# A four-layer graph network: block 1 is turned behind block 0 in layer zero, its products follow the second unit, and layer one's prologue gets a second square buffer

## The chip, the cores and the metric

The kernel runs on one core of one Trainium2 chip. TensorE (PE) multiplies matrices into PSUM, VectorE (DVE), ScalarE (ACT) and GpSimd (POOL) work element by element, and SyncE (SP) issues most of the transfers. The metric is device time in microseconds of one launch; a time is the median of several executions. One further execution was recorded by the hardware profiler. Its clock starts at the start of the recorded span.

## The reference, cut to what matters

Four graph layers run one after the other over 4096 nodes with 256 features each, under one dense 4096 x 4096 adjacency of 0 and 1. Each layer computes new features from the neighbours, adds them to the old ones and normalises each row.

```python
# layer 0: additive attention, 4 heads       x = layernorm(x + elu(softmax(leaky(s_i + s_j), masked) @ (x @ W)))
# layer 1: dot-product attention, 4 heads    q, k, v = x @ Wq + bq, x @ Wk + bk, x @ Wv + bv
#                                            x = layernorm(x + softmax(q k^T / 8 + mask^T) @ v)
# layer 2: additive attention, 1 head        as layer 0, with one head and another slope
# layer 3: cosine attention                  x = layernorm(0.5 * softmax(cos(k, q), masked) @ x + 1.5 * x)
x = _layernorm(x + _L0_gnn_ref(x, adj, L0_gnn_W, L0_gnn_a), axis=-1)
x = _layernorm(x + _L1_gnn_ref(x, adj, L1_gnn_Wq, ...), axis=-1)
```

All of it is float32. Layers are counted from zero here, as in the names of the inputs; the change's own short description counts layer 1 of the code as the second.

## The kernel before, in words

The features stay in SBUF as `X`, 32 tiles of 128 rows, in eight blocks of four tiles (512 rows). A product that contracts over the features needs a block turned, so that features lie on partitions. There are two ways of turning one in this kernel. `transposed_block` (L112) does it with eight PE transposes of 128 x 128 into two PSUM banks, each copied out into `xT` by an engine that the caller names. `turning_apart` (L122), called through `block_apart` (L151), does it without PE: DVE transposes 32 x 32 squares into a buffer `squares` (two instructions, L129), one DMA writes that to DRAM (`far`, L133), and four DMAs read it back with the squares in their turned places (L137).

**Layer zero** (`additive_heads`) goes over units (block b of targets, tile j of sources), 8 x 32 of them. For a unit, `weights` (L291) lets ACT compute four heads of unnormalised weights from a broadcast row (L299, four instructions), and DVE adds one and multiplies by the mask (L302, one instruction of 128 x 2048). `sums` (L305) then multiplies the values of tile j with these weights on PE (L312), two units later (`LAG = 2`). Ahead of that stand the values. For each block, `turn` (L354) turns the features and asks for the load of the block after next, and `prepare` (L361) calls `additive_values` (L208): PE multiplies with the weights `w_sb` (L215; three tiles into the PSUM tile `side`, one into another bank), ACT takes three exponentials of each part (L219 to L221) and DVE scales the values (L222, one instruction for three tiles and one for the fourth).

The start is written out. PE runs two small products of ones (`warm`, L377), broadcasts `a_row` into `side`, DVE attaches the attention vectors to the weights (L107, L109), block 0 is turned, two more products of ones follow, block 0's values are prepared, and `first_rows` (L267) broadcasts block 0's source terms into four banks: one of its own and three of the PSUM tile `over`. The first unit's weights read these banks, and `keep_rows` (L275) copies them into SBUF, two by ACT and two by DVE (L277). Then block 1 is turned into two banks of `side`, and the loop begins. In step i = 0, behind unit 0's weights, block 2 is turned and block 1 prepared.

**Layer one** (`multi_head_attention`) begins with projections. `keys(b)` multiplies block b by Wk and Wq on PE (L738), ACT adds the bias (L746), and DVE takes the greatest absolute value of each part (L747). `values(b)` does the same for Wv (L757, L764). Between `keys(0)` and `keys(1)` stands `tail`, the end of layer zero's last block: DVE divides and takes negatives (L329, L331, L229), ACT the exponential (L230), DVE adds and normalises. Block 1 is turned on PE with copies by ACT (L119), blocks 2 to 7 through DRAM, with one buffer for `squares` (pool `mh_sq`, L718), two for `far` and four for `xT`. Then come 8 x 64 units of attention. Layers two and three follow; neither is touched.

PE's order is the order of the code wherever `manual_schedule` names PE, which covers both places. The order on DVE, ACT and SP in these two places is chosen when the kernel is built, by a scheduler that places the instructions by estimated readiness. [...] A tile of a pool can be written again when the last reader of its former content is done.

## Time and profile before

| | us |
|---|---|
| median of 3 executions | 2790.39 (2789.6 to 2793.18) |
| profiled execution, its own time | 2791.86 |
| its span | 2790.1 |
| PE busy | 2772.4 |
| DVE busy | 2286.1 |
| ACT busy | 1702.6 |
| POOL busy | 1051.2 |
| layer zero's products begin | 19.37 |
| layer one's projections begin | 722.69 |
| layer one's attention begins | 812.45 |

The granted TensorE clock was 0.999 over the profiled execution. In a timeline of the profile each row gives the start, the length, the engine, the line, the operation, what it writes and reads, and in brackets the idle time of that engine just before it with what ended this. A list of waits gives the sum, the number of times and the longest. A 32-bit product appears as two records, a transpose as one.

### The profile page before, as it was taken

To read this page: it belongs to the slowest core of one execution; us is meant where nothing else is said; L and a number is where in the kernel's file an instruction comes from. 1 tells how busy PE (TensorE), PEld (TensorE's weight loads), DVE (VectorE), ACT (ScalarE), POOL (GpSimd) and SP (SyncE) were. 2 spreads that over 40 slices of the span, in tenths; PEclk is the share of its full clock that TensorE was granted. 3 is DMA by queue.
4 is the path that set the end of the run, shared out by engine and by line. 5 is a ranking of instruction groups with operands and counts; after the bars stand their busy time and mean duration, and the time that the engine had idled before them with its cause. 6 is when DMAs were issued, how large, how long until landed. Compare 5 with 4: busy or idle time off the path is not lost. (4 is left out here: it accounts for less than half of the span.)

```text
span 2790.1 us, 50215 instructions
## 1 busy us (share of the span) xinstructions
PE 2772.4 (99%) x19445; PEld 1427.4 (51%) x19445; DVE 2286.1 (82%) x3055; ACT 1702.6 (61%) x2665; POOL 1051.2 (38%) x986
## 2 busy tenths in 40 slices
PE   9999999999999999999999999999999999999999
PEld 5333333333453333333333333688888777777776
DVE  8899999999677788887888888888887877767676
ACT  8899999999336666666666666465565422222222
POOL 0000001100029878778788784355455000000000
PEclk9999999999999999999999999999999999999999
DMA  7566676665339899998989988567777545445442
GB/s 209 109 140 137 139 145 132 135 142 114 69 97 193 184 179 196 192 188 183 195 181 190 191 182 187 169 195 215 186 210 232 117 77 82 76 68 83 75 72 43
DMA packets 275065, 411.92 MB, mean 148 GB/s; under 512 B 54809, under 2 KB 155657, under 8 KB 273930
## 3 DMA queue, kind: packets, MB, share of 16 engines
q0 software_dynamic: 104176, 182.74, 41.3%
q1 hardware_dynamic: 164280, 218.88, 26.3%
q10 hardware_dynamic: 6370, 7.10, 0.7%
q8 instruction: 152, 2.49, 0.4%
q14 instruction: 87, 0.71, 0.1%
HBM read 335.94 MB, written 39.40 MB: 135 GB/s over the span
## 5 line engine op out<-in xcount | busy, mean ns | idle before, releaser
L837 DVE TENSOR_TENSOR prob<-p,mask 128x1024 f32<-128x1024 f32 x512 | 619.8, 1222 | 166.9 <-ACT p L827 160.7
L827 ACT ACTIVATE p<-p,shift 128x1024 f32<-128x1024 f32 x512 | 555.6, 1088 | 318.9 <-PE p L825 318.7
L312 PE MATMUL acc<-prob,V 128*32 128x512 f32 x6144 | 664.0, 592 | 1.2 <-DVE prob L302 1.2
L299 ACT ACTIVATE prob<-row,dst 128x512 f32<-128x512 f32 x1020 | 635.1, 712 | 0.6
L302 DVE SCALAR_TENSOR_TENSOR prob<-prob,mask 128x2048 f32<-128x2048 f32 x256 | 580.4, 2286 | 25.8 <-ACT prob L299 25.2
L847 POOL TENSOR_TENSOR den<-den,prob 128x1024 f32<-128x1024 f32 x220 | 558.2, 2537 | 91.1 <-DVE prob L837 84.1
L825 PE MATMUL p<-qT,kT 64*64 64x512 f32 x4096 | 531.1, 590 | 1.6 <-DVE prob L837 1.6
L861 PE MATMUL acc<-prob,V 64*64 64x512 f32 x4096 | 529.9, 589 | 0.0
L312 PEld LDWEIGHTS acc<-prob,V 128*32 128x32 f32 x6144 | 197.3, 110 | 453.0 <-issue 431.6
L446 PE MATMUL acc<-mix,mixed 128*128 128x256 f32 x1428 | 388.6, 380 | 4.3 <-DVE mix L437 1.3
L861 PEld LDWEIGHTS acc<-prob,V 64*64 64x64 f32 x4096 | 157.4, 133 | 282.1 <-issue 280.3
L825 PEld LDWEIGHTS p<-qT,kT 64*64 64x64 f32 x4096 | 154.3, 133 | 278.6 <-issue 256.1
L446 PEld LDWEIGHTS acc<-mix,mixed 128*128 128x128 f32 x1428 | 269.3, 190 | 47.6 <-PE acc L446 3.5
L90 POOL COPY tick<-prob 128x1 f32<-128x1 f32 x35 | 38.0, 1085 | 642.1 <-DVE prob L302 641.2
L1133 DVE TENSOR_TENSOR prob<-prob,mask 128x1024 f32<-128x1024 f32 x128 | 156.1, 1219 | 145.9 <-ACT prob L1125 145.8
L853 POOL DMA_DIRECT2D den<-prob x240 | 230.3, 960 | 62.5 <-DMA den<-prob 22.3
L1053 POOL DMA_DIRECT2D mask<-in_adjT x64 | 47.6, 743 | 530.5 <-DVE prob L1133 442.4
L446 PE MATMUL acc<-prob,X 128*128 128x256 f32 x952 | 244.3, 379 | 0.0
L446 PEld LDWEIGHTS acc<-prob,X 128*128 128x128 f32 x952 | 180.8, 190 | 78.1 <-issue 56.4
L569 DVE SCALAR_TENSOR_TENSOR prob<-r,own,mask 128x512 f32<-128x512 f32 x252 | 177.1, 743 | 51.4 <-POOL s L169 13.6
L1125 ACT ACTIVATE prob<-p 128x512 f32<-128x512 f32 x144 | 86.1, 598 | 204.0 <-PE p L1121 204.0
L1125 ACT ACTIVATE prob<-g 128x512 f32<-128x512 f32 x112 | 66.9, 597 | 208.0 <-PE g L1121 208.0
(236 smaller groups left out, 2821.9 us busy)
## 6 DMA issues: line engine op xcount, KB each, us to landing
mask<-in_adjT SPq DMA_DIRECT2D x254, 512.0 KB
den<-prob POOLq DMA_DIRECT2D x240, 512.0 KB, 5.3
mask<-edges SPq DMA_DIRECT2D x512, 64.0 KB
mask<-in_adjT POOLq DMA_DIRECT2D x64, 512.0 KB, 5.7
edges<-in_adj POOLq DMA_DIRECT2D x32, 512.0 KB, 9.6
far<-squares SPq DMA_DIRECT2D x16, 512.0 KB
den<-prob SPq DMA_DIRECT2D x16, 512.0 KB
row<-far SPq DMA_DIRECT2D x7, 1024.0 KB
```

What stands on the lines that cost most here:

```text
L299: nc.scalar.activation(z[:, h, :], r, AF.Relu, bias=-1.0, scale=dst[:, j, h:h + 1])
L302: nc.vector.scalar_tensor_tensor(z, z, 1.0, mask[m][:, j % MJ, :].unsqueeze(1).to_broadcast([P, H, QW]), OP.add, OP.mult)
L312: nc.tensor.matmul(acc[b][h * G:(h + 1) * G, n, :], part, prob[b, j][:, h, :], start=(j == 0), stop=(j == NT - 1))
L446: nc.tensor.matmul(acc[at][:, half * HW:(half + 1) * HW], w, a, start=(g == 0 and n in (0, 2, 3, 5)), stop=(g == NP - 1), skip_group_check ...
L569: nc.vector.scalar_tensor_tensor(z[:, n, :], r, ga.own[:, j:j + 1], mask[:, n, :], OP.add, OP.mult)
L825: nc.tensor.matmul(p[c * d:(c + 1) * d, r, :], kT[half, c, at:at + d], qT[half, c, cols], start=True, stop=True)
L827: nc.scalar.activation(p, p, AF.Exp, bias=shift)
L837: nc.vector.tensor_tensor(z, p, mask[m][:, j % MJ, :].unsqueeze(1).to_broadcast([P, KC, QW]), OP.mult)
L847: nc.gpsimd.tensor_tensor(to, to, flat, OP.add)
L853: nc.gpsimd.dma_start(to, flat, accum_op=OP.add)
L861: nc.tensor.matmul(acc[b][c][r * d:(r + 1) * d, :], V[half, j, r * d:(r + 1) * d], prob[b, j][half, r, :], start=(j == 0), stop=(j == NH - 1))
L1133: nc.vector.tensor_tensor(z, z, co.mask[b, 2 * g // MJ][:, lo:lo + 2, :], OP.mult)
```

## The change

Block 1's transposes move up behind block 0's, into two banks of `over`, in the place of the second pair of warm-up products; these two go. Both of its copies out of PSUM go to ACT, where they were DVE's. In the loop, turning block 2 and preparing block 1 move from step i = 0 to step i = 1, so in the code they stand behind the second unit's weights. The first products (`sums`) still come in step 2, so that PE's own order from `first_rows` on stays, but for the eight transposes that have moved. In layer one's prologue the pool of the square buffers gets two buffers.

```diff
--- before.py
+++ after.py
@@ -354,8 +354,7 @@
             def turn(b, bank=bank):
                 if b + 2 < NB:
                     load_x(b + 2)
-                busy = (nc.scalar.copy if b == 0 else nc.vector.tensor_copy,
-                        nc.vector.tensor_copy if b == 1 else nc.scalar.copy)
+                busy = (nc.scalar.copy if b < 2 else nc.vector.tensor_copy, nc.scalar.copy)
                 xTs[b] = transposed_block(sb, bank, b, busy)
 
             def prepare(b):
@@ -380,12 +379,11 @@
                 nc.tensor.matmul(side[:, 0, :], ones[:1, :], a_row, start=True, stop=True)
                 attach(keep, w_sb, side[:, 0, :], H)
                 turn(0)
-                warm(2)
+                free = iter([over[:, 1, :], over[:, 2, :]])
+                turn(1, lambda: next(free))
                 prepare(0)
                 banks = [bank()] + [over[:, h, :] for h in range(H - 1)]
                 first_rows(banks)
-                free = iter([side[:, 0, :], side[:, 1, :]])
-                turn(1, lambda: next(free))
                 for i in range(len(units) + LAG):
                     if i < len(units):
                         b, j = units[i]
@@ -400,8 +398,8 @@
                         if b:
                             finish(b - 1, j)
 
-                    if i == 0 or i % QB == 3 and 3 + i // QB <= NB:
-                        b = 1 if i == 0 else 2 + i // QB
+                    if i == 1 or i % QB == 3 and 3 + i // QB <= NB:
+                        b = 1 if i == 1 else 2 + i // QB
                         if b + 1 < NB:
                             turn(b + 1)
                         prepare(b)
@@ -715,7 +713,7 @@
             with ExitStack() as pro:
                 wp = pool(pro, "mh_w", 1)
                 sb = pool(pro, "mh_in", 4)
-                sq = pool(pro, "mh_sq", 1)
+                sq = pool(pro, "mh_sq", 2)
                 own = pool(pro, "mh_o", 2)
                 dr = pool(pro, "mh_far", 2, space=bass.MemoryType.DRAM)
                 ps = pool(pro, "mh_ps", 6, space=PSUM)
```

In the order built from this, DVE's copies of block 1 are gone, its copy of block 2 stands ahead of the first copied row, and the scaled values of block 1's fourth tile stand behind unit 1's mask step. In layer one's prologue the squares of blocks 3, 4 and 5 stand ahead of the first reciprocal of layer zero's last block, where only block 3's stood, and SP has the square writes of blocks 2 to 5 ahead of the reads of block 2, where it had those of blocks 2 and 3. What follows is unchanged on every engine.

## The prediction

> **What bounds the kernel now.** I read the page first, for the engine that is never idle. Its part on busy time:

> ```profile
> PE 2772.4 (99%) x19445; PEld 1427.4 (51%) x19445; DVE 2286.1 (82%) x3055; ACT 1702.6 (61%) x2665; POOL 1051.2 (38%) x986
> ```

> TensorE (PE) is busy for 2772.4 of 2790.1 us: 17.7 us of idle time in all. Only moving PE's few waits can change the time. So the second view is the list of PE's waits (in total, times, longest); four touch the edited places:

> ```profile
> PE g L738 <- ACT xT L119: 1.4, 1, 1.4
> ...
> PE acc L312 <- DVE prob L302: 1.2, 1, 1.2
> ...
> PE acc L215 <- DVE xT L119: 0.5, 1, 0.5
> PE pv L757 <- DVE V L764: 0.3, 1, 0.3
> ```

> Two lie in the first 26 us, two in layer one's projections near 737 us. The third view is the timeline of each engine there. PE at the start (start, length, engine, operation; idle time before it in brackets):

> ```profile
> 4.26 2.05 PE L117 MATMUL g<-ident,X 128*128 128x128 f32 x8
> 6.11 1.06 PE L377 MATMUL acc<-ones 128*128 128x128 f32 x4
> 7.45 3.12 PE L215 MATMUL acc<-w_sb,xT 128*128 128x264 f32 x12 [0.29 <-issue]
> ...
> 13.19 1.04 PE L117 MATMUL acc<-ident,X 128*128 128x128 f32 x8
> ...
> 23.30 2.78 PE L312 MATMUL acc<-prob,V 128*32 128x512 f32 x24 [1.16 <-DVE prob L302]
> ```

> The same eight transposes take 2.05 us at 4.26 and 1.04 us at 13.19. The last row is the one that matters: unit 1's products wait for VectorE's mask step (L302). VectorE (DVE) up to it:

> ```profile
> 14.27 1.29 DVE L119 COPY xT<-acc 128x512 f32<-128x512 f32 x2 [2.01 <-PE acc L117]
> 15.77 0.69 DVE L277 COPY row<-acc 128x512 f32<-128x512 f32 x1 [0.21 <-ACT prob L299]
> 16.37 2.28 DVE L302 SCALAR_TENSOR_TENSOR prob<-prob,mask 128x2048 f32<-128x2048 f32 x1
> 18.57 0.69 DVE L277 COPY row<-acc 128x512 f32<-128x512 f32 x1
> 19.17 0.68 DVE L119 COPY xT<-g 128x512 f32<-128x512 f32 x1
> 19.77 0.95 DVE L222 TENSOR_TENSOR V<-acc,V 128x768 f32<-128x768 f32 x1
> 20.64 0.42 DVE L222 TENSOR_TENSOR V<-g,V 128x256 f32<-128x256 f32 x1
> ```

> Unit 1's mask step follows at 20.97. In layer one, DVE, ACT and PE around PE's 1.4 us wait:

> ```profile
> 732.44 1.30 DVE L129 STREAM_TRANSPOSE squares<-X 128x512 f32<-128x512 f32 x2 [6.26 <-DMA far<-squares]
> 733.67 0.64 DVE L747 TENSOR_REDUCE kbig<-kT 128x1 f32<-128x512 f32 x1
> ...
> 735.97 0.28 DVE L229 TENSOR_SCALAR neg<-o 128x256 f32<-128x256 f32 x1
> ...
> 736.28 0.42 ACT L230 ACTIVATE neg<-neg 128x256 f32<-128x256 f32 x1 [5.33 <-DVE neg L229]
> 736.61 1.05 ACT L119 COPY xT<-g 128x512 f32<-128x512 f32 x2
> ...
> 737.23 3.70 PE L738 MATMUL g<-xT,wk_sb 128*128 128x512 f32 x8 [1.36 <-ACT xT L119]
> ```

> DVE sits 6.26 us because block 3's squares need the one square buffer, which block 2's write to DRAM still reads. DVE's negatives of layer zero's last block stand behind it, ScalarE's (ACT) exponential behind those, ACT's copies of block 1's features behind that, and PE at the end.

> [...] (2.05 against 1.04 us), so transposes put in place of the second warm-up keep the array as busy, and run slow. [...] GpSimd's transfer of the first mask, issued at 723.11 and landing 6.7 us later, fills the engines while block 2's squares wait; these move at up to 469 GB/s only from about 728 and land by 732.4. [...]

> **The change part by part**, with the built order of each engine: PE changes only at the start; in layer one DVE and SP change, ACT does not.

> Start, PE. Out goes the second warm-up (6.11 to 7.17, and 0.29 idle); eight transposes of block 1 come in, and leave their place at 13.19, a saving of 0.88 us there (to the next at 14.07). They need block 1's load, third on SP's queue. The DMA rates of the first microseconds sum to the 1.31 MB of block 0, w0 and block 1 at about 6.2 us; with some landing time, 6.4. At the cold pace 1.85 us to the next instruction: block 0's products start at 8.25 and not 7.45. Their first group took 3.12 us against 2.84 later, so 0.2 comes back: first rows 0.6 us later (0.2 if the load is there at 6.11, 1.5 if it lands at 7.3).

> Start, ACT and DVE. Two copies (2 x 0.59) go to ACT, which is idle from 6.94 to 10.61: free. DVE loses 2 x 0.69, which delayed nothing but the row copy at 15.77 by little, as that then waited for ACT. Unit 0's mask step follows ACT's weights: 16.37 + 0.6 = 16.97. From unit 0's to unit 1's mask step DVE takes 4.60 us now. Afterwards block 2's copy stands before the first row copy, in time that DVE waits anyway, and the one-tile V product behind unit 1's mask step (this is what products behind the second weights do; PE's own order there stays). Left: 2.20 + 0.60 + 0.87 = 3.67. Unit 1's mask step: 20.64 against 20.97, **0.3 us gained** (bounds: 0.7 gained, 0.6 lost). PE has no further wait until layer one's projections, so this reaches them whole.

> Layer one. With two buffers block 3's squares (two of 0.61) follow block 2's at once, at 724.7, during DVE's idle time: free. But in the built order blocks 4's and 5's squares come forward too, before the reciprocal at 734.82. Block 4's need the landing of block 2's write, so they start at 732.44, as block 3's did. Block 5's need block 3's write. That is issued near 726.1 and not 733.8; its data goes right behind block 2's, so about 733.6, and DVE asks at 734.24: no further wait. So four transposes stand behind the old wait where two stood: 2 x 0.61 = 1.22 us more ahead of DVE's negatives, and every link to PE is exposed. PE's wait grows from 1.36 to about 2.6: **1.2 us lost**. Bounds: nothing lost and 1.36 gained, if block 2's write lands 2.6 us earlier; 1.8 lost if block 3's write takes as long as the uncrowded ones (2.4 us from issue at 756.08 to use at 758.81) after block 2's landing. PE's 0.3 us wait moves with DVE and stays. Later squares (1.57 and 3.58 us of DVE waits) go; no PE wait stood behind those.

> SP is the queue passed. It issues four square writes and then 16 reads, each instruction in turn, instead of two and eight. Block 2's reads go from 734.29 to about 736. Ahead of them 1.05 MB of blocks 4 and 5 and then their own 0.52 at some 230 GB/s (what that queue moved from 734 to 740): landed by about 743, and PE wants them at 748.57. Free, with 6 us of cover.

> The sum: -0.3 + 1.2 = +0.9 us on a span of 2790.1. The profiled execution took 2791.86, the median is 2790.39: **2791.3 us**, no change that can be told, since 0.2% (5.6 us) is about what a measurement of this kernel tells from no change; the three runs alone spread over 3.6.

> **Rivals.** (a) The wait leaves layer one: block 2's write lands early enough that four transposes end before PE notices. For: block 3's write no longer starts late, and POOL's mask is not tied to it. Against: the first mask's issue follows PE's last product of layer zero in both kernels. Price: -0.3 - 1.4 = 2788.7. (b) The start loses: block 1's load lands near 8, first rows come 2 us later and unit 1's mask step 1.1 us later: +1.1 + 1.2 = 2792.7. For: the load shares the engines with w0; against: the sum of bytes above. (c) Slower: block 3's write is held up behind two transfers, and DVE's second wait goes to PE one to one. It decides the sign when the write lands 4.7 us after 734.24, at 739; at 740 the time is 0.9 + 5.8, 2797.1. For: block 2's took 7.65 us from its issue; against: the mask that held it is done by 729.8. (d) The edit does nothing: the second buffer is never used ahead. The built order speaks against it; the start's +-0.5 alone would be left, 2790.1.

> **How the numbers follow.** The forecast 0.60 (its own range, with the scatter of runs, 2789.5 to 2793); (a) 0.12, (b) 0.13, (d) 0.05: all within 0.2%. (c) 0.07. Something faster by over 0.2% that no wait here allows (the four waits and the warm-up sum to 4.5 us): 0.03. So faster 0.03, same 0.90, slower 0.07. Range 2788.6 to 2794.5: it takes in (a), (b) and the bounds of the forecast, and leaves (c) out.

> **What would show it.** Right: PE's wait at L738 near 2.6 us; in layer one DVE's wait on the squares' write ending near 732.4, followed by two transposes, a reduction and two more; unit 1's products starting near 23.0 with no wait at block 1's products. Wrong: a second DVE wait between the square pairs (c), a PE wait at the second eight transposes above 1 us (b), L738 without a wait (a), any new wait after 749 us, where I expect none.

## The result: 2796.9 us, slower by some 2 to 5 us, and the profile after

| | before | after | ratio after/before |
|---|---|---|---|
| first comparison, median of 12 and 12 executions, us | 2791.52 (2789.47 to 2796.3) | 2796.94 (2792.9 to 2799.79) | 1.0016 [1.0009, 1.0024] |
| the changed kernel once more, median of 31 and 19, us | 2793.36 (2789.74 to 2799.25) | 2796.92 (2792.45 to 2800.41) | 1.0008 [1.0001, 1.0015] |
| profiled execution, its own time, us | 2791.86 | 2795.52 | |
| its span, us | 2790.1 | 2793.7 | |

The change makes the kernel slower, by 0.08% to 0.16%, which is 2.2 to 4.5 us; the medians lie 3.6 and 5.4 us apart. That is inside the 0.2% named as no change, but both intervals exclude 1. The predicted 2791.3 is below every execution of the changed kernel, and the range ended at 2794.5. The two profiled executions differ by 3.7 us where 0.9 was forecast, so 2.8 us must be found in the trace. Part of the miss against 2791.3 is not the change at all: the median of the unchanged kernel was 2790.39 in the three executions that the prediction had, and 2791.52, 2794.54 and 2793.36 in the later comparisons.

Busy time, from the page of the changed kernel:

```profile
PE 2773.0 (99%) x19441; PEld 1427.6 (51%) x19441; DVE 2289.1 (82%) x3053; ACT 1703.8 (61%) x2667; POOL 1052.7 (38%) x986
```

PE is busy for 0.6 us more than before, and idle for 2793.7 - 2773.0 = 20.7 us in place of 17.7. So most of the loss is waits. The list of PE's waits of the changed kernel (total, times, longest):

```profile
PE g L736 <- ACT xT L119: 2.3, 1, 2.3
PE acc L117 <- DMA X<-in_x: 2.0, 1, 2.0
PE acc L312 <- DVE row L277: 1.5, 1, 1.5
```

L736 is the former L738. Its wait grew from 1.36 to 2.30 us, near the 2.6 foreseen. A wait on block 1's load (L117), for which the forecast had a landing at 6.4 us and so some 0.3, is 2.0 us, and unit 0's products have a new wait of 1.5 us. PE's timeline of the changed kernel, over both places:

```profile
4.21 1.97 PE L117 MATMUL g<-ident,X 128*128 128x128 f32 x8
8.21 1.97 PE L117 MATMUL acc<-ident,X 128*128 128x128 f32 x8 [2.02 <-DMA X<-in_x]
9.97 3.65 PE L215 MATMUL acc<-w_sb,xT 128*128 128x264 f32 x12
...
22.36 2.78 PE L312 MATMUL acc<-prob,V 128*32 128x512 f32 x24 [1.52 <-DVE row L277]
25.59 2.78 PE L312 MATMUL acc<-prob,V 128*32 128x512 f32 x24 [0.45 <-DVE prob L302]
...
740.46 3.70 PE L736 MATMUL g<-xT,wk_sb 128*128 128x512 f32 x8 [2.30 <-ACT xT L119]
```

Read the starts against those before. Block 0's products: 9.97 for 7.45, 2.5 us late. Unit 1's products: 25.59 for 23.30, 2.3 late. Keys of block 1: 740.46 for 737.23, 3.2 late. The spans: 3.6. So nearly two thirds of the loss arise in the first 26 us, one more microsecond at L736, and the rest is within what PE's small waits change from one execution to the next. Now DVE, in the same execution:

```profile
18.81 0.69 DVE L277 COPY row<-acc 128x512 f32<-128x512 f32 x1 [1.24 <-ACT prob L299]
19.42 2.28 DVE L302 SCALAR_TENSOR_TENSOR prob<-prob,mask 128x2048 f32<-128x2048 f32 x1
21.62 0.68 DVE L277 COPY row<-acc 128x512 f32<-128x512 f32 x1
22.22 0.95 DVE L222 TENSOR_TENSOR V<-acc,V 128x768 f32<-128x768 f32 x1
23.24 2.29 DVE L302 SCALAR_TENSOR_TENSOR prob<-prob,mask 128x2048 f32<-128x2048 f32 x1
...
734.49 1.31 DVE L129 STREAM_TRANSPOSE squares<-X 128x512 f32<-128x512 f32 x2 [5.69 <-DMA far<-squares]
735.72 0.64 DVE L745 TENSOR_REDUCE kbig<-kT 128x1 f32<-128x512 f32 x1
736.28 1.29 DVE L129 STREAM_TRANSPOSE squares<-X 128x512 f32<-128x512 f32 x2
...
739.20 0.28 DVE L229 TENSOR_SCALAR neg<-o 128x256 f32<-128x256 f32 x1
```

Unit 0's mask step begins at 19.42 and not at 16.37; unit 1's follows 3.82 us later and not 4.60. The second copy of a row (21.62) is what unit 0's products wait for, because their tile takes the place of `over` in the pool, and that copy reads from `over`. This wait costs nothing by itself, since unit 1's products wait for unit 1's mask step in either case. In layer one four transposes stand behind the old wait, in the order foreseen: two, a reduction, and two more without a second wait. DVE ran nothing of what stood behind the first pair while it waited for 5.69 us.

### The profile page after: what moved, and what is told of

It is laid out like the page before. It is cut to its first block, busy times and chain, and to the rows that moved or that the text cites. A ratio compares the mean times of both kernels' runs of the same rounds, so it can differ in the third digit from the quotient of the medians.

```text
span 2793.7 us, 50203 instructions
## 1 busy us (share of the span) xinstructions
PE 2773.0 (99%) x19441; PEld 1427.6 (51%) x19441; DVE 2289.1 (82%) x3053; ACT 1703.8 (61%) x2667; POOL 1052.7 (38%) x986
## 5 line engine op out<-in xcount | busy, mean ns | idle before, releaser
L312 PE MATMUL acc<-prob,V 128*32 128x512 f32 x6144 | 664.0, 592 | 2.0 <-DVE row L277 1.5
L299 ACT ACTIVATE prob<-row,dst 128x512 f32<-128x512 f32 x1020 | 634.8, 712 | 0.6
L302 DVE SCALAR_TENSOR_TENSOR prob<-prob,mask 128x2048 f32<-128x2048 f32 x256 | 580.5, 2286 | 25.6 <-ACT prob L299 24.8
L312 PEld LDWEIGHTS acc<-prob,V 128*32 128x32 f32 x6144 | 197.3, 110 | 453.9 <-issue 431.6
```

Of the source, the lines that this page charges most:

```text
L299: nc.scalar.activation(z[:, h, :], r, AF.Relu, bias=-1.0, scale=dst[:, j, h:h + 1])
L302: nc.vector.scalar_tensor_tensor(z, z, 1.0, mask[m][:, j % MJ, :].unsqueeze(1).to_broadcast([P, H, QW]), OP.add, OP.mult)
L312: nc.tensor.matmul(acc[b][h * G:(h + 1) * G, n, :], part, prob[b, j][:, h, :], start=(j == 0), stop=(j == NT - 1))
```

## The experiments

In the tables of starts, "unit 1" is the start of unit 1's products, the point where the start of the kernel hands its delay on to everything after. Single executions come with one time each; their verdict rests on the trace, not on that time.

### The two halves of the change apart

The start alone is the changed kernel with one square buffer, as the diff has it; the squares alone are the kernel before with two, the same line the other way round.

```diff
-                sq = pool(pro, "mh_sq", 2)
+                sq = pool(pro, "mh_sq", 1)
```

> The changed start with one square buffer. Theory A (two separate losses: block 1's load lands near 8.2 us and costs about 2.3 us at the start, the squares moved ahead cost about 0.9 in layer one): PE waits 1.5 to 2.5 us before the second eight transposes, unit 1's products start near 25.6 against 23.3, the wait at layer one's second keys stays at 1.4, and the median is 2.3 us over before. Rival B (the start costs only what one execution happened to show, and the rest of the 5.4 us between the medians comes with the second buffer, or from a stage that neither edit touches): no more than 1 us over before.

> The old start with two square buffers. Theory A: the first 26 us as before, PE's wait at layer one's second keys 2.3 us against 1.4, the median 0.9 us over before. Rival B: 3 us or more over before, with idle time of PE that lies outside the first 26 us and the projections.

PE's timelines of the start alone, and of the squares alone:

```profile
7.78 1.97 PE L117 MATMUL acc<-ident,X 128*128 128x128 f32 x8 [1.26 <-DMA X<-in_x]
9.55 3.86 PE L215 MATMUL acc<-w_sb,xT 128*128 128x264 f32 x12
...
25.36 2.78 PE L312 MATMUL acc<-prob,V 128*32 128x512 f32 x24 [0.44 <-DVE prob L302]
```

```profile
738.43 5.33 PE L738 MATMUL g<-xT,wk_sb 128*128 128x512 f32 x8 [2.53 <-ACT xT L119]
...
750.49 3.60 PE L738 MATMUL g<-xT,wk_sb 128*128 128x512 f32 x8
```

| | unit 1 | wait at the second keys | second keys |
|---|---|---|---|
| before | 23.30 | 1.36 | 737.23 |
| start alone | 25.36 | 1.20 | 739.13 |
| squares alone | 23.33 | 2.53 | 738.43 |
| both | 25.59 | 2.30 | 740.46 |

By the second keys the start has lost 1.90 us, the squares 1.20, and both 3.23: they nearly add up. The squares' 1.2 us is the forecast's figure.

One execution says little of a start, so take all of them: unit 1's products begin at 23.30 to 24.70 in the five executions with the start as before (23.76 in the mean), and at 25.36 to 27.00 in the three with the changed one (25.98). The two groups don't overlap, and the 2.2 us between their means is the start's loss as the traces show it. The timed medians can't confirm losses of this size: 2794.73 for the start alone (14 executions), 2794.67 for the squares alone (13), against 2794.54 (27) for the kernel before on the same chip, ratios 1.0000 [0.9993, 1.0008] and 1.0004 [0.9997, 1.0012]. An interval of 0.0015 is 4 us wide. The 2.3 us over before that was expected of the start alone is not in its median, which is 0.2 us over; it lies at the upper end of the interval, some 2.2 us. What follows rests on the traces.

The squares alone lost more behind the second keys. These took 5.33 us and not 3.70, since the granted clock was 0.50 from 738.33 to 741.74, and the third keys begin at 750.49 against 748.57: 1.92 us lost by then. In every trace here the changes of the granted clock lie whole multiples of 3.413 us apart (one from 738.33 to 741.74; 814 from full pace at 7.89 us to half clock at 2786.33, after PE's last work, in the kernel before, and 814 from 11.61 to 2790.06 in the changed one); call that a step. The step before this one held 2.43 us of PE idle time. The start alone shows the same once, far from both edits: 2.68 us of idle time in one step, then half clock from 2510.17 to 2513.58. No other step between full pace and PE's last work holds more than 1.81 us in any of the fourteen profiled executions, and none of them was followed by half clock. The waits of the changed kernel at L736, 2.30 and 2.97 us, each fell across two steps, and no half clock followed. So such a wait can cost more in one execution than in another. How often it does in the timed executions is not shown.

### Is it the early turn, or the order on DVE

The start alone again, with block 0's products ahead of block 1's turn. The second warm-up stays away.

```diff
                 turn(0)
+                prepare(0)
                 free = iter([over[:, 1, :], over[:, 2, :]])
                 turn(1, lambda: next(free))
-                prepare(0)
```

> The changed start, one square buffer, but block 1 is turned behind block 0's products and not ahead of them. Theory A (the load is late): PE no longer waits for a load; the products of block 0 start at about 7.4, the turning costs 0.9 us ahead of the first rows, and unit 1's products start at 23.0 to 23.6. If the loss came from the copies on ScalarE instead, they would hold unit 0's weights as before, and unit 1's products would still start after 25.

```profile
7.46 4.97 PE L215 MATMUL acc<-w_sb,xT 128*128 128x264 f32 x12 [1.08 <-ACT xT L119]
...
25.65 2.78 PE L312 MATMUL acc<-prob,V 128*32 128x512 f32 x24 [0.44 <-DVE prob L302]
```

No wait for the load is left, the products start where they did before (7.46), and still unit 1 begins at 25.65. The twelve records took 4.97 us, where before they took 3.12. The load's wait was thus only one way to lose those 2 us. Here PE stood idle for 1.08 us where the warm-up had been, and full pace, seen in the single records of the trace (0.223 us for a record of 264 columns instead of 0.44), began at 11.55 us instead of 7.96. By itself this start after 25 us also fits the rival named beforehand, that block 1's copies on ACT hold up unit 0's weights; the run with the warm-up put back, further down, has the same copies and answers it.

### The load with nothing behind it

The start alone, with no later load of features, mask or edges issued until DVE has attached the attention vectors to the weights (a small DVE copy of these into block 2's place opens the queue again, at 8.31 us). The core of the edit; the first masks and edges are held in the same way:

```diff
-                if b + 2 < NB:
-                    load_x(b + 2)
+                if 1 < b < NB - 2:
+                    with tc.issue_after(first[0]):
+                        load_x(b + 2)
```

> The changed start, one square buffer; the loads of blocks 2 and 3, of the first mask and of all that follows wait until VectorE has attached the vectors to the weights (about 8 us), so that nothing stands on SP's queue behind block 1's load. If that load is late because later loads share the DMA engines with it, it lands at 6.3 to 6.8 and PE waits 0.6 us at most. If it is late because its sixteen parts run on engines of unequal progress whatever follows, PE still waits 1.5 to 2.2 us. Units 0 and 1 may start later here, as their mask and block 2 come later.

```profile
6.99 1.97 PE L117 MATMUL acc<-ident,X 128*128 128x128 f32 x8 [0.68 <-DMA X<-in_x]
8.75 4.17 PE L215 MATMUL acc<-w_sb,xT 128*128 128x264 f32 x12
...
24.89 2.78 PE L319 MATMUL acc<-prob,V 128*32 128x512 f32 x24 [0.44 <-DVE prob L309]
```

With the queue to itself, block 1's load lets the transposes begin at 6.99 us; with the later loads behind it, at 7.78, 8.21 and 8.58 in the three executions that waited for it with the queue unchanged. In the second of these, the first profile of the changed kernel, the load's sixteen parts landed from 6.21 to 8.16 us. PE's wait is 0.68 us, where at most 0.6 was expected if the later loads are the cause, and 1.5 to 2.2 if they are not. So, by this one execution, between 0.8 and 1.6 us of its lateness are the transfers behind it. What remains is 0.8 us over the 6.2 us of the sum of bytes; the queue moved next to nothing after 6.3 us, so some 0.7 us lie between the last bytes and their first use. But unit 1's products begin at 24.89, only 0.47 us sooner than in the start alone, since the twelve records now took 4.17 us: full pace came at 11.65.

### The warm-up put back

First, the order with block 0's products ahead, and `warm(2)` back in front of them, as the diff has it. Second, the start alone with only a `warm(4)` added between the two turns, so that PE is busy while the load is awaited.

```diff
                 turn(0)
+                warm(2)
+                prepare(0)
                 free = iter([over[:, 1, :], over[:, 2, :]])
                 turn(1, lambda: next(free))
-                prepare(0)
```

> As the run with the later turning, one square buffer, and the second pair of warm-up products is back ahead of block 0's products. Theory A (the idle microsecond before about 7.9 us costs TensorE its full pace until about 11.4): block 0's first twelve records take 3.1 us again and not 4.97, first rows start at 12.2 to 12.4 and not 14.03, unit 1's products at 23.6 to 24.0 and not 25.65. Theory B (those records were slow because they waited for the weights or for a copy): no more than 0.5 us earlier than without the warm-up.

> The changed start with block 1 turned ahead of block 0's products, one square buffer, and four warm-up products between the two turnings, to keep TensorE busy while block 1's load is under way. Theory A: the load still decides when the second turning starts (7.5 to 8.3), but that takes 1.0 us and not 2.0, and block 0's first twelve records 2.9 to 3.1 and not 3.65; unit 1's products start at 23.8 to 24.5, against 25.4 to 25.6. Theory B: the same as without them, 25.4 to 25.6.

PE's timelines, the first and the second:

```profile
6.38 1.06 PE L376 MATMUL acc<-ones 128*128 128x128 f32 x4
7.38 2.91 PE L215 MATMUL acc<-w_sb,xT 128*128 128x264 f32 x12
...
23.52 2.78 PE L312 MATMUL acc<-prob,V 128*32 128x512 f32 x24 [0.45 <-DVE prob L302]
```

```profile
6.33 1.92 PE L376 MATMUL acc<-ones 128*128 128x128 f32 x8
8.04 1.91 PE L117 MATMUL acc<-ident,X 128*128 128x128 f32 x8
9.74 3.14 PE L215 MATMUL acc<-w_sb,xT 128*128 128x264 f32 x12
...
24.85 2.78 PE L312 MATMUL acc<-prob,V 128*32 128x512 f32 x24 [0.44 <-DVE prob L302]
```

With 1.06 us of filler back and block 1's turn behind the products, unit 1 begins at 23.52 instead of 25.65: nearly all of the start's loss is gone (before: 23.30), in an execution whose full pace came early, at 7.38, the earliest of all. ACT makes the same copies here, so these were not what held the start. In the second, no PE gap is left, and the records take 3.14 us in place of 3.86. Yet unit 1 begins at 24.85, later than the 23.8 to 24.5 expected, as full pace came only at 10.18 us: a PE that is always busy is not all that it hangs on.

### Do transposes bring PE to full pace

The kernel before, with forty transposes of block 0's tiles, read by nobody, in place of the second warm-up.

```diff
-                warm(2)
+                for k in range(40):
+                    nc.tensor.transpose(over[:, 0, k % QB * P:(k % QB + 1) * P], X[:, k % QB, :P], ident)
```

> The kernel before, with forty transposes of block 0's tiles (whose results nothing reads) in place of the second warm-up. No instruction of PE waits for a load between 4.2 us and the products. Full pace has begun at 7.4 to 11.3 us in the eight executions whose PE had no gap before the first products, and at 11.55 to 13.9 us in the five that had one. Theory one, the gap of PE delays full pace and transposes keep the array as busy as products do: the forty begin near 6.3 us at 0.213 us each, and somewhere between 7.4 and 11.3 us they go over to 0.107 us; they are done between 10.7 and 13.1 us, and block 0's first twelve product records come at full pace, in about 2.8 us. Theory two, [...] all forty take 0.213 us, 8.5 us in all, the products begin near 14.8 us, and full pace comes only 1.7 to 4.1 us after that, so that the twelve records take 3.6 to 5 us. The time itself is 3 to 10 us over that of the kernel before.

```profile
6.37 5.18 PE L384 MATMUL acc<-ident,X 128*128 128x128 f32 x40
11.38 2.84 PE L215 MATMUL acc<-w_sb,xT 128*128 128x264 f32 x12
```

All forty at the slow pace would be 8.5 us. They took 5.18: the first seven come 0.213 us apart, from about 7.7 us on they are 0.109 us apart, and the products run at full pace from their first record. So in this execution PE went over to full pace in the middle of a row of transposes, after 3.5 us of nothing but transposes (4.22 to 7.7 us). The price is clear too: the single time is 2796.89 against 2792.01, with unit 1 at 26.95.

The records give the moment of full pace, to within one record, in each of the fourteen profiled executions. Nine had no gap over 0.5 us before the first products: 7.38, 7.7, 7.96, 7.99, 8.36, 8.87, 10.18, 10.43, 11.34. Five had a gap of 0.68 to 2.33 us there: 11.55, 11.65, 11.67, 11.68, 13.86. The two groups don't overlap. The clock's change to full pace is on record too, so the steps of 3.413 us seen above can be counted back from it in each execution. The step that ended with this change held at most 0.32 us of PE idle time in all fourteen, and at most 0.65 us of the one-row product that broadcasts `a_row`. Every step before it held at least 0.42 us of idle time or at least 0.69 us of that product. So full pace came at the end of the first step that PE had filled almost wholly with other work. No step with a gap of 0.7 us or more inside it ended with that change. Where the steps begin differed from one execution to the next: less whole steps, the fourteen moments above lie some 0.2 to 3.4 us after the start of the span. This is read from fourteen records with narrow margins, and no run could set where the steps begin.

### The squares kept out of DVE's way

The kernel before with two square buffers, and the squares of blocks 4 and later allowed only after the step that ends layer zero's last block (`ends` holds the instructions that scale a finished row).

```diff
-                            xTs[b + 1] = block_apart(sb, sq, dr, b + 1, nc.sync)
+                            with tc.issue_after(ends[-1]) if b > 2 else nullcontext():
+                                xTs[b + 1] = block_apart(sb, sq, dr, b + 1, nc.sync)
```

> The old start and two square buffers, but the squares of blocks 4 and on are queued on VectorE behind the last scaled row of layer zero's last block. If the loss in layer one is the four transposes and the old wait ahead of the negatives: VectorE waits for no transfer there, the wait of 1.4 us at layer one's second keys (2.5 with two buffers) is gone or under 0.3, and the second keys start at 735.9 and not 737.2. If it is something else about the second buffer, 2.3 us or more remain.

```profile
725.46 1.89 DVE L129 STREAM_TRANSPOSE squares<-X 128x512 f32<-128x512 f32 x3
...
733.15 0.28 DVE L232 TENSOR_SCALAR neg<-o 128x256 f32<-128x256 f32 x1
```

```profile
724.10 4.11 PE L741 MATMUL g<-xT,wk_sb 128*128 128x512 f32 x8
...
737.11 3.60 PE L741 MATMUL g<-xT,wk_sb 128*128 128x512 f32 x8
...
747.43 3.60 PE L741 MATMUL g<-xT,wk_sb 128*128 128x512 f32 x8
```

DVE no longer waits for a write ahead of the negatives, the wait of 1.36 us at the second keys is gone, and so is the 0.31 us wait of the values behind them. From the first keys to the third PE takes 747.43 - 724.10 = 23.33 us where the kernel before took 748.57 - 722.69 = 25.88: 2.55 us gained, 1.53 of it before the second keys. (These begin at 737.11 and not at the expected 735.9, as the start of this execution was late.) The second buffer with this order is worth 2.55 us, and without it it gives 1.2 us away. The same order with one buffer was not run, so how much of the gain needs the second one is open.

### What made block 2's write late

The kernel before with the first mask's transfer held back into layer one's attention, so that it is issued at about 1662 us and not at 723, once with one square buffer and once with two.

```diff
-                    nc.gpsimd.dma_start(ga.first_mask, adjT.rearrange("(t p) i -> p t i", p=P)[:, :QB, :QW])
+                    with behind(prob[b + 1, j][:, 0, :1]):
+                        nc.gpsimd.dma_start(ga.first_mask, adjT.rearrange("(t p) i -> p t i", p=P)[:, :QB, :QW])
```

> The old start and one square buffer; only GpSimd's transfer of layer two's first mask is held back, to block 7 of layer one's attention. If that transfer is what keeps block 2's squares on their way for 7.6 us: VectorE's wait on it ends near 728 and not at 732.4, and PE's wait at the second keys goes from 1.4 to under 0.3. If the write takes that long by itself, nothing changes in layer one's prologue.

> Two square buffers in their built order (squares of blocks 4 and 5 ahead of the negatives) with layer two's first mask held back, old start. If the four transposes cost their 1.2 us only where they stand behind a late transfer: the old wait ends near 730, the negatives come 1.2 us later than with one buffer and the mask held back (733.5), at 734.7, and PE waits at most 0.4 at the second keys. If the second buffer costs something more, 1 us or more of waiting there.

DVE with one buffer, and then with two:

```profile
729.97 1.30 DVE L129 STREAM_TRANSPOSE squares<-X 128x512 f32<-128x512 f32 x2 [3.38 <-DMA far<-squares]
```

```profile
729.81 1.30 DVE L129 STREAM_TRANSPOSE squares<-X 128x512 f32<-128x512 f32 x2 [2.83 <-DMA far<-squares]
731.60 1.29 DVE L129 STREAM_TRANSPOSE squares<-X 128x512 f32<-128x512 f32 x2
734.52 0.28 DVE L229 TENSOR_SCALAR neg<-o 128x256 f32<-128x256 f32 x1
```

The wait that ended at 732.44 now ends near 730, from 7.65 us after the write's issue to 4.8. So the first mask accounts for some 2.8 us, which is more than PE's wait: with either number of buffers that wait is gone. With one buffer PE goes from 723.10 to 746.42 between the first keys and the third:

```profile
723.10 4.10 PE L738 MATMUL g<-xT,wk_sb 128*128 128x512 f32 x8
...
736.10 3.60 PE L738 MATMUL g<-xT,wk_sb 128*128 128x512 f32 x8
...
746.42 3.60 PE L738 MATMUL g<-xT,wk_sb 128*128 128x512 f32 x8
```

That is 23.32 us, the same gain as with the squares held, and it needs no second buffer. It isn't free: PE waits 4.0 us for the tiles of L837, in layer one's attention, in both runs, where no other run has more than 2.6. The late end of the write was a surprise, since I had expected 728. Most of its bytes were moved by 727.3, and the last came at no more than 27 GB/s.

### The good parts together

The squares held, two buffers, and block 1's products in step i = 1, as the change has it; the start's turn and warm-up as they were before. Beside the ordering constraint shown above it has this edit, and it ran next to the changed kernel.

```diff
-                    if i == 0 or i % QB == 3 and 3 + i // QB <= NB:
-                        b = 1 if i == 0 else 2 + i // QB
+                    if i == 1 or i % QB == 3 and 3 + i // QB <= NB:
+                        b = 1 if i == 1 else 2 + i // QB
```

> Meant to beat both: the old start with block 1's turning and copies where they were, but block 1's products behind the second unit's weights; two square buffers, with the squares of blocks 4 and on behind the last scaled row. From the steps that held: unit 1's products start at 22.9 to 23.0 and not 23.3, the waits of 1.4 and 0.3 us in layer one are gone. Together 2.0 us under before, a ratio of 0.9993, about as much as the interval is wide.

> The changed kernel once more. If its loss is the sum of the two places that the profile shows (2.3 us in the first 26, 0.9 to 1.2 in layer one): 3.2 to 3.5 us over before, a ratio of 1.0011 to 1.0013. If the 5.4 us between the first medians is the true size, a ratio near 1.0019, and idle time of PE beyond 850 us that the kernel before hasn't.

DVE and PE of the kernel with the good parts:

```profile
18.20 2.28 DVE L305 SCALAR_TENSOR_TENSOR prob<-prob,mask 128x2048 f32<-128x2048 f32 x1
...
22.46 2.28 DVE L305 SCALAR_TENSOR_TENSOR prob<-prob,mask 128x2048 f32<-128x2048 f32 x1
```

```profile
7.73 4.66 PE L218 MATMUL acc<-w_sb,xT 128*128 128x264 f32 x12 [0.29 <-issue]
...
24.80 2.78 PE L315 MATMUL acc<-prob,V 128*32 128x512 f32 x24 [0.82 <-DVE prob L305]
...
737.20 3.60 PE L741 MATMUL g<-xT,wk_sb 128*128 128x512 f32 x8
```

And PE of the changed kernel, profiled once more:

```profile
8.58 1.97 PE L117 MATMUL acc<-ident,X 128*128 128x128 f32 x8 [2.33 <-DMA X<-in_x]
10.34 4.70 PE L215 MATMUL acc<-w_sb,xT 128*128 128x264 f32 x12
...
742.54 3.70 PE L736 MATMUL g<-xT,wk_sb 128*128 128x512 f32 x8 [2.97 <-ACT xT L119]
```

The good parts give 2791.9 us (2787.88 to 2793.95, 13 executions), 5.0 below the changed kernel and 1.5 below the kernel before in the same comparison; the latter's ratio, 0.9994 [0.9986, 1.0002], doesn't tell it from no gain. In its trace the projections keep their gain (747.52 - 724.19 = 23.33 us from first to third keys), and the distance of the mask steps is 4.26 and not 4.60 us. The expected start near 22.9 was missed by almost 2 us: full pace came at 11.34, with the start of the kernel before. One execution of an unchanged start can lose nearly as much as the change's early turn did, which also says how little one profile tells of the start. The changed kernel's second profile has the same two losses, both larger: the load at 8.58, full pace at 13.86, L736 at 2.97. Its ratio in the table at the top, 1.0008 [1.0001, 1.0015], is near the 1.0011 to 1.0013 that these two losses would give, and its interval leaves out the 1.0019 of the first medians.

## Why the prediction was wrong, by its own steps

**What bounds the kernel, right.** Every difference found sits in PE's waits or in PE's pace in the places named, and after the second keys little is added (3.2 us there, 3.6 in the spans).

**Start, PE: wrong, and this is the step that failed.** "The DMA rates of the first microseconds sum to the 1.31 MB [...] at about 6.2 us; with some landing time, 6.4." PE could use the load at 8.21. First rows were put 0.6 us later; unit 0's mask step, which follows them, came 3.05 us later. The load is 1.8 of the 2.4 us missed, and about 0.65 is the pace: twelve records in 3.65 us where I had taken some 2.9. That the wait for the load itself puts off full pace had no term in the sum. The upper bound, a landing at 7.3, was passed wherever the transposes waited with later loads behind theirs; only alone on its queue was the load there at 6.99. The sum of bytes gives the time by which so many bytes of all transfers have moved (the last of these were used 0.8 us after it even with the queue empty behind them). It says nothing on whose bytes they are, and the loads of later blocks were on the same queue right behind.

**"Transposes put in place of the second warm-up keep the array as busy": true of transposes, false here.** It was an assumption that no run had tested; the forty transposes, at full pace from about 7.7 us, bear it out. The eight of the change could not, because they were not there yet: the warm-up that went had no operand to wait for, and they had. A filler was exchanged for an instruction that waits. Nor had the prediction a measured time for full pace: from PE's first product at 1.06 us it took 6.3 us at the least, and up to 12.8.

**Start, DVE, right.** From unit 0's to unit 1's mask step 3.67 us was predicted and 3.82 measured, against 4.60. This gave back 0.78 of the 3.05 us. The "0.3 us gained" turned into 2.3 us lost at the start (2.1 in the run of the start alone).

**Layer one, right.** Four transposes behind the old wait, no second wait, 1.2 us lost: 1.17 with the squares alone, 0.94 and 1.61 in the two profiles of the changed kernel. That these waits are long enough for a step at half clock, as the squares alone had one, was not foreseen. That the mask's transfer holds the write is borne out, for 2.8 us of its lateness. SP's queue cost nothing, as claimed: no PE wait on the reads appeared.

**The rivals.** (b) had the mechanism, a load "near 8" with first rows 2 us later, and was given 0.13 for a sum of bytes that spoke against it. Its price of 1.1 us was half of what the start lost, for want of the pace. Its sign, a PE wait above 1 us at the second eight transposes, came with 2.02 us. (a), (c) and (d) didn't happen. With the right start, 2.3 + 1.2 = 3.5 us on 2791.86 is 2795.4, and the profiled execution took 2795.52. So close a fit is partly luck: the kernel before was profiled with the earliest start of the five.

**The range, too narrow for a second reason.** It hung on three executions that spread over 3.6 us. Later the same kernel spread over 9.5 in one comparison (2789.74 to 2799.25), with medians 4 us apart from one comparison to the next. "Within 0.2%" held; a range of 6 us could not.

## What to carry to other kernels

A sum of bytes says when so much has been moved, not when one load has landed: for an instruction that would wait for a load, read where its bytes stand among those queued right behind it, and keep the early work behind work that has no such operand. A warm-up in front of the first products is not filler to be traded for useful instructions, unless these can start at once. When a pool gets a second buffer, look at what the scheduler will now draw forward and in front of what; a buffer that loses by itself can win with one ordering constraint. And profile a start several times before reading a microsecond from it.
